# A gated cross-attention block on one core: softmax sums moved into the next group, longer due times for the feed-forward steps, a new order for the first sample and for the last group

## Chip, cores and metric

The kernel runs on one core of one Trainium2 chip. The metric is the device time of one execution in microseconds (us); lower is better. The kernel before was timed in three runs: 2811.11, 2811.09 and 2810.47 us, median 2811.09 us. One further execution was profiled; it took 2809.42 us, and its trace spans 2807.6 us from the first to the last instruction.

## What is computed

Four samples (B = 4) of 256 rows by 512 features (`x`) attend to 1601 context rows each (`ctx_kv`), then pass a feed-forward part with routed low-rank experts. Everything is float32.

```python
x = x + tanh(g_xattn) * xattn(layernorm(x), ctx, Wq, bq, Wkv, bkv, Wo, bo)
x = x + tanh(g_ffn)   * ffn(layernorm(x), base_W, router_W, lora_A, lora_B)

# xattn: 8 key/value heads, 4 query heads on each, head size 128
q = (query @ Wq + bq);  k, v = split(ctx @ Wkv + bkv)
attn = softmax(q k^T / sqrt(128));  out = (attn v) @ Wo + bo

# ffn: a base product and two of eight low-rank experts (rank 16)
probs = softmax(x @ router_W^T);  w = top-2 of probs, normalised
out = x @ base_W^T + 2 * sum_e w_e * (x @ lora_A_e) @ lora_B_e
```

## The kernel before

**Tiles.** A "head" below is one sample and one of its 8 key/value heads: 32 heads in all. Each head has two "groups" (`l` = 0, 1), of 128 rows of `x` with the 4 query heads that share the key: W = 512 columns. So there are 64 groups. The 1601 context rows are cut into 13 tiles of 128 rows (KT = 13); the last has 65 rows. For the softmax they are taken in 7 units (`pairs`): the 65-row tile alone first, then six units of two tiles.

**A group.** A score matmul (line 416, tile `sc`) multiplies the keys of one context tile with the 512 query columns. TensorE runs a float32 matmul in two passes, so 13 tiles are 26 matmul records. ScalarE copies each score tile from PSUM into an SBUF tile `p` (line 423), and VectorE folds the copies into a running maximum (`fold`, lines 373 to 378). `softmax` (line 430 on) then spreads the maximum over the partitions (`spread`), subtracts it from every `p` (line 437), lets ScalarE take the exponential (line 438), folds the running sum in the same loop, and spreads the sum's reciprocal. The value product (line 453, tile `av`) uses these `p` tiles in the next group's section: `run_group(cur, prev)` alternates score units of the current group with value units of the one before, which trail by AHEAD = 3 units. There are NBUF = NPAIR + AHEAD = 10 `p` tiles. VectorE multiplies the value product with the reciprocal sum (line 463), ScalarE adds the value bias (line 464), and an output projection (line 476, tile `po`) adds into the residual `xa`.

**Order of TensorE.** TensorE's order is written out by the program; the other engines' orders are chosen when the program is compiled. A small planner keeps a virtual clock (`clock["now"]`) that advances by an assumed cost for each TensorE step (`mm_cost`: 857 ns for a two-pass 512-column matmul). Work outside the score and value units is put into `Task` lists: key and query projections of the next head (`qk_steps`, tiles `pk` and `pq`), value projections (`v_steps`, tile `pv`), the output projection, the feed-forward steps, and transposes of the next sample's context. Each step has a cost and a lag: it is due only that long after the step ahead of it. `run_group` may run one due step of up to 432 ns after each unit; `fill`, after each group, runs due steps up to a share of what is left; `flush` runs a set to its end, and moves the clock forward where nothing is due. A lag that is too short lets TensorE reach an instruction whose input isn't there, and everything behind it in TensorE's queue waits.

**Feed-forward.** After a sample's last head, `ffn_steps` gives four steps for each 128-row part: a layer norm on VectorE (`fn`), its transpose on TensorE (`pt_f`, LAG_NORM = 6000 ns later), the router and expert product `pm` with a chain of about twenty small VectorE instructions that ends in `mid` (lines 524 to 548), and, LAG_ROUTE = 13000 ns later, `final_item`: the transpose of `mid` (line 558), the base product `py` (line 563) and the expert product into the same bank (line 564).

**Beginning and end.** The first sample's 13 context tiles are loaded into `p` tiles by SyncE's and ScalarE's DMA queues in turn, behind the biases and the first key weights; `x` goes in after the fourth. They are transposed (`pt_ctx`) and copied to `ctxT` by VectorE (line 143), layer norms of `x` come between, and the four blocks of key matmuls follow as their chunks are complete. The value projection follows the first group's scores. At the end the last group's value units run alone, after its softmax.

Of the kernel before, what the change touches and what calls it, by code (L numbers as in the profile page):

```python
# [27 lines left out]
def flamingo_kernel(  # L28
# [55 lines left out]
    AHEAD = 3  # L84
# [25 lines left out]
    nc.gpsimd.dma_start(gates[:, 0:1], g_xattn.partition_broadcast(P))  # L110
    nc.gpsimd.dma_start(gates[:, 1:2], g_ffn.partition_broadcast(P))
    nc.scalar.activation(gates, gates, AF.Tanh)
    tgx, tgf = gates[:, 0:1], gates[:, 1:2]
    bo_b = const.tile([P, D], F32, name="bo_b")
    nc.gpsimd.dma_start(bo_b, bo.partition_broadcast(P))
# [4 lines left out]
    nc.sync.dma_start(bias[0:NHEAD], bq.rearrange("(h p) -> h p", p=P))  # L120
    nc.sync.dma_start(bias[NHEAD:], bkv.rearrange("(h p) -> h p", p=P))
    biasT = const.tile([P, NBIAS], F32, name="biasT")
    pb = bank("pb")
    nc.tensor.transpose(pb[:, :NBIAS], bias, ident[:NBIAS, :NBIAS])
    nc.vector.tensor_copy(biasT, pb[:, :NBIAS])
# [12 lines left out]
    def transpose_rows(src, n, dst, name):  # L138

        pt = bank(f"pt_{name}").rearrange("p (c k) -> p c k", k=P)  # L140
        for c in range(NC):
            nc.tensor.transpose(pt[:, c, :n], src[:n, c * P : (c + 1) * P], ident[:n, :n])  # L142
        nc.vector.tensor_copy(dst, pt[:, :, :n])  # L143
# [23 lines left out]
    def load_wk(b, h):  # L167
        k = pool.tile([P, NC, HDIM], F32, tag="wk", name=f"wk_{b}_{h}")
        nc.sync.dma_start(
            k, wkv[:, h * HDIM : (h + 1) * HDIM].rearrange("(c p) f -> p c f", p=P)  # L170
        )
        w_t["k", b, h] = k

    def load_wv(b, hp):
        v = pool.tile([P, NC, 2 * HDIM], F32, tag="wv", name=f"wv_{b}_{hp}", bufs=1)
        lo = KVD + hp * 2 * HDIM
        nc.sync.dma_start(v, wkv[:, lo : lo + 2 * HDIM].rearrange("(c p) f -> p c f", p=P))
        w_t["v", b, hp] = v
# [47 lines left out]
    LAG_DMA, LAG_CTX, LAG_NORM, LAG_ROUTE = 2500, 1500, 6000, 13000  # L226
    LAG_EVAC, LAG_O, LAG_SOFTMAX = 1500, 6000, 12000
# [52 lines left out]
    def turn_ctx(b, i, src):  # L280
        transpose_rows(src, rows[i], ctxT_t[b][:, :, i * P : i * P + rows[i]], f"ctx_{b}_{i}")
# [120 lines left out]
    def score_unit(key, j):  # L402
# [4 lines left out]
        def run():  # L407
# [3 lines left out]
            p = pool.tile([P, 2, W], F32, tag="p", name=f"p_{nm}_{j}", bufs=NBUF)  # L411
# [16 lines left out]
    acc_t = {}  # L428

    def softmax(key):  # L430
        nm = "_".join(map(str, key))
        mb = spread(acc_t[key], ALU.max, f"mx_{nm}")
        sm = pool.tile([P, 2, W], F32, tag="sm", name=f"sm_{nm}", bufs=1)
        for j, tiles in enumerate(pairs):
# [4 lines left out]
            fold(sm, ALU.add, j, key)  # L439
        rb_t[key] = spread(sm, ALU.add, f"sm_{nm}", lambda m: nc.vector.reciprocal(m, m))  # L440
# [52 lines left out]
    def ffn_steps(b, l):  # L493
# [26 lines left out]
        def route_item():  # L520
            pm = bank(f"pm_{nm}")
            WR = E * R + E
            for c in range(NC):
                nc.tensor.matmul(
                    pm[:, :WR], box["xT"][:, c, :], ra[:, c, :], start=(c == 0), stop=(c == NC - 1)
                )
            lm = pool.tile([P, WR], F32, tag="lm", name=f"lm_{nm}")
# [28 lines left out]
        def final_item():  # L556
# [4 lines left out]
            py = bank(f"py_{nm}")  # L561
            for c in range(NC):
                nc.tensor.matmul(py, box["xT"][:, c, :], base_t[:, c, :], start=(c == 0), stop=False)  # L563
# [8 lines left out]
            (NC * mm_cost(E * R + E), LAG_EVAC, route_item),  # L572
            ((NC + 1) * mm_cost(D), LAG_ROUTE, final_item),
# [4 lines left out]
    NBUF = NPAIR + AHEAD  # L578
# [29 lines left out]
    def flush(which, until=math.inf):  # L608

        while left := [t for t in tasks if which(t)]:  # L610
            t = min(left, key=lambda t: max(t.ready, clock["now"]))
            if t.ready > until:
                break
# [3 lines left out]
    def run_group(cur, prev):  # L617
# [3 lines left out]
        for j in range(NPAIR + AHEAD):  # L621
            if cur is not None and j < NPAIR:
                units.append(score_unit(cur, j))
            if prev is not None and j >= AHEAD:
                units.append(av_unit(prev, j - AHEAD))
        for cost, fn in units:
            fn()
            clock["now"] += cost
            if (t := next_task(NC * TR_COST)) is not None:
                t.step()  # L630
# [3 lines left out]
    def fill(share, wait=LAG_EVAC):  # L634

        credit = share * sum(t.cost() for t in tasks)
        while tasks and credit > 0:
            if (t := next_task()) is None:
                soon = min(t.ready for t in tasks)
                if soon > clock["now"] + wait:  # L640
                    break
# [10 lines left out]
    load_wk(*heads[0])  # L652
    staged = {}
    for i in range(KT):
        eng = nc.sync if i % 2 == 0 else nc.scalar
        if i % 2 == 0:
            two = pool.tile([P, 2, W], F32, tag="p", name=f"ctx_0_{i}", bufs=NBUF)
        staged[i] = two[:, i % 2, :]
        eng.dma_start(staged[i][: rows[i]], ctx_kv[0, i * P : i * P + rows[i], :])
        if i == 3:  # L660
            xs = x_steps(0, 0)
            xs.pop(0)[2]()
    load_wq(*heads[0])
    load_wv(0, 0)
# [3 lines left out]
    done = 0  # L668
    for (s, n), k in zip(chunks, ks):
        while done * P < s + n:  # L670
            turn_ctx(0, done, staged.pop(done))
            done += 1
        if xs:
            for f in xs[:2]:
                f[2]()
            xs = xs[2:]
        k[2]()
    for f in qs:
# [4 lines left out]
    tasks.append(Task(v_steps(0, 0), (0, 0)))  # L683

    prev = None
    for hi, (b, h) in enumerate(heads):
# [9 lines left out]
        if nxt is not None:  # L696
            ks, qs = qk_steps(*nxt)
            if nxt[1] == 0:
                tasks.append(Task(ctx_steps(nxt[0]) + ks + v_steps(nxt[0], 0) + qs, nxt))
                tasks.append(Task(x_steps(nxt[0], LAG_NORM), nxt))  # L700
            else:
# [5 lines left out]
        for l in range(NL):  # L707
            cur = (b, h, l)
            fill(0)
# [4 lines left out]
            if hi == 0 and l == 0:  # L714
                flush(lambda t: t.head == heads[0])
                tasks.append(Task(ffn_weight_steps()))
            fill(1.0 / (NL - l), LAG_EVAC if nxt is not None else LAG_SOFTMAX)
# [3 lines left out]
    flush(lambda t: True, clock["now"] + LAG_SOFTMAX)  # L721
    run_group(None, prev)
    tasks.insert(0, Task(out_steps(prev)))
    flush(lambda t: True)
# [43 lines left out]
```

## Time and profile before

| what | value |
|---|---|
| median of three runs (range) | 2811.09 us (2810.47 to 2811.11) |
| the profiled execution / its span | 2809.42 us / 2807.6 us |
| TensorE (PE) busy, share of the span | 2708.2 us, 96% |
| VectorE (DVE) busy | 2034.1 us, 72% |
| ScalarE (ACT) busy | 1152.8 us, 41% |
| DMA over the span | 104.53 MB, mean 37 GB/s |
| mean granted TensorE clock | 0.986 |

How to read it: the page gives busy time per engine, the chain of work that ended last, and groups of instructions by source line. The list of waits says which engine stood before an instruction and what released it; the timeline lists instructions in order of time, where like ones are merged ("x4") with the start of the first and the time from there to the end of the last. A matmul's recorded end is modelled and overlaps the next one's start, so the spacing of starts is what counts. "PEld" is the load of the stationary operand. A busy TensorE can still be a slow one: its granted clock (1.00 is full) stands beside each window.

### The profile page before, as it was taken

To read this page: it belongs to the slowest core of one execution; us is meant where nothing else is said; L and a number is where in the kernel's file an instruction comes from. 1 tells how busy PE (TensorE), PEld (TensorE's weight loads), DVE (VectorE), ACT (ScalarE), POOL (GpSimd) and SP (SyncE) were. 2 spreads that over 40 slices of the span, in tenths; PEclk is the share of its full clock that TensorE was granted. 3 is DMA by queue.
4 is the path that set the end of the run, shared out by engine and by line. 5 is a ranking of instruction groups with operands and counts; after the bars stand their busy time and mean duration, and the time that the engine had idled before them with its cause. 6 is when DMAs were issued, how large, how long until landed. Compare 5 with 4: busy or idle time off the path is not lost.

```text
span 2807.6 us, 22670 instructions
## 1 busy us (share of the span) xinstructions
PE 2708.2 (96%) x7997; PEld 1469.5 (52%) x7997; DVE 2034.1 (72%) x3146; ACT 1152.8 (41%) x1769; POOL 6.2 (0%) x21
## 2 busy tenths in 40 slices
PE   7999999999899999999999999999999999999995
PEld 4655555555545555555544555555554455555542
DVE  4676777787658777768756787677866667777785
ACT  2443443443334434434433444344433434443442
POOL 0000000000000000000000000000000000000000
PEclk9999999999999999999999999999999999999997
DMA  4100010111101101102010111011210101110000
GB/s 149 42 34 27 34 34 23 42 53 47 45 26 37 39 19 42 34 23 71 29 45 27 42 34 34 27 34 38 61 36 23 36 25 34 41 34 15 31 15 8
DMA packets 69801, 104.53 MB, mean 37 GB/s; under 512 B 3068, under 2 KB 27692, under 8 KB 69688
## 3 DMA queue, kind: packets, MB, share of 16 engines
q1 hardware_dynamic: 68552, 100.99, 11.2%
q10 hardware_dynamic: 864, 1.57, 0.2%
q8 instruction: 63, 1.03, 0.1%
q0 software_dynamic: 272, 0.53, 0.1%
q14 instruction: 50, 0.41, 0.0%
HBM read 100.98 MB, written 2.10 MB: 37 GB/s over the span
## 4 chain that ended last, share of the span: by engine, by line
PE 86%; DVE 11%; issue 1%; ACT 1%; DMA 1%; ACTq 0%; DVEq 0%
PE sc L416 26%; PE av L453 23%; PE pv L347 11%; PE pk L295 10%; PE pq L314 7%; PE po L476 6%; DVE p L437 3%; DVE sm L378 2%; PE py L563 1%; ACT p L423 1%; DVE mx L378 1%; DVE sm L373 1%; DVE ctxT L143 0%; DMA xa<-in_x_dram 0%; PE pt_ctx L142 0%
## 5 line engine op out<-in xcount | busy, mean ns | idle before, releaser
L416 PE MATMUL sc<-qT,kT 128*128 128x512 f32 (+1 forms) x1664 | 783.8, 604 | 4.8 <-ACT qT L321 4.5
L453 PE MATMUL av<-p,v 128*128 128x512 f32 (+1 forms) x1664 | 759.3, 594 | 0.0
L423 ACT COPY p<-sc 128x512 f32<-128x512 f32 (+1 forms) x832 | 461.8, 587 | 710.1 <-PE av L453 607.0
L378 DVE TENSOR_TENSOR mx<-mx,p 128x1024 f32<-128x1024 f32 x256 | 313.3, 1224 | 442.2 <-ACT p L423 441.8
L453 PEld LDWEIGHTS av<-p,v 128*128 128x128 f32 (+1 forms) x1664 | 315.1, 191 | 386.9 <-issue 386.4
L416 PEld LDWEIGHTS sc<-qT,kT 128*128 128x128 f32 (+1 forms) x1664 | 292.5, 186 | 419.9 <-issue 273.8
L438 ACT ACTIVATE p<-p 128x1024 f32<-128x1024 f32 (+1 forms) x448 | 440.2, 994 | 127.1 <-DVE p L437 120.3
L437 DVE TENSOR_TENSOR p<-p,res_mx 128x1024 f32<-128x1024 f32 (+1 forms) x448 | 489.9, 1139 | 1.9
L347 PE MATMUL pv<-wv,ctxT 128*128 128x256 f32 (+1 forms) x1664 | 370.8, 380 | 0.0
L295 PE MATMUL pk<-ctxT,wk 128*128 128x400 f32 (+1 forms) x1024 | 357.3, 501 | 5.9 <-DVE ctxT L143 5.9
L347 PEld LDWEIGHTS pv<-wv,ctxT 128*128 128x128 f32 (+1 forms) x1664 | 310.2, 186 | 64.4 <-issue 15.3
L378 DVE TENSOR_TENSOR sm<-sm,p 128x1024 f32<-128x1024 f32 x256 | 311.9, 1218 | 11.2 <-ACT p L438 0.5
L295 PEld LDWEIGHTS pk<-ctxT,wk 128*128 128x128 f32 x1024 | 193.4, 190 | 167.5 <-issue 23.5
L476 PE MATMUL po<-wo,oT 128*128 128x512 f32 x512 | 233.8, 600 | 4.9 <-ACT oT L464 4.9
L314 PE MATMUL pq<-xnT,wq 128*128 128x256 f32 x1024 | 233.5, 382 | 0.0
L314 PEld LDWEIGHTS pq<-xnT,wq 128*128 128x128 f32 x1024 | 195.3, 191 | 43.5 <-issue 11.0
L464 ACT ACTIVATE oT<-oT,biasT 128x512 f32<-128x512 f32 x64 | 46.2, 722 | 371.6 <-DVE oT L463 371.6
L373 DVE TENSOR_TENSOR mx<-p,p 128x1024 f32<-128x1024 f32 x64 | 77.1, 1205 | 138.7 <-ACT p L423 138.7
L354 ACT COPY v<-pv 128x512 f32<-128x512 f32 (+1 forms) x112 | 61.7, 552 | 239.8 <-PE pv L347 239.8
L476 PEld LDWEIGHTS po<-wo,oT 128*128 128x128 f32 x512 | 98.2, 192 | 111.5 <-issue 94.6
L302 ACT ACTIVATE kT<-pk,biasT 128x400 f32<-128x400 f32 (+1 forms) x128 | 74.3, 584 | 74.7 <-PE pk L295 74.7
L321 ACT ACTIVATE qT<-pq,biasT 128x256 f32<-128x256 f32 x128 | 58.7, 463 | 61.3 <-PE pq L314 60.8
(96 smaller groups left out, 1124.9 us busy)
## 6 DMA issues: line engine op xcount, KB each, us to landing
wq<-in_L_xattn_Wq_dram SPq DMA_DIRECT2D x32, 1024.0 KB, 5.2
wo<-in_L_xattn_Wo_dram SPq DMA_DIRECT2D x32, 1024.0 KB, 5.1
ctx<-in_ctx_dram SPq DMA_DIRECT2D x42, 256.0 KB, 2.7
wk<-in_L_xattn_Wkv_dram SPq DMA_DIRECT2D x32, 256.0 KB, 3.1
wv<-in_L_xattn_Wkv_dram SPq DMA_DIRECT2D x16, 512.0 KB, 3.3
xa<-in_x_dram SPq DMA_DIRECT2D x4, 512.0 KB, 6.0
out_dram<-y SPq DMA_DIRECT2D x8, 256.0 KB, 2.6
ctx<-in_ctx_dram ACTq DMA_DIRECT2D x6, 256.0 KB, 5.1
```

The source lines that it names most:

```text
L295: nc.tensor.matmul(pk[:, :n], w_t["k", b, h][:, c, :], ctxT_t[b][:, c, s : s + n], start=(c == 0), stop=(c == NC - 1),)
L302: nc.scalar.activation(kT_t[b, h][:, s : s + n], pk[:, :n], AF.Identity, bias=bias_of("k", h),)
L314: nc.tensor.matmul(pq[:, :L], w_t["q", b, h][:, c, g * HDIM : (g + 1) * HDIM], xnT_t[b][:, c, :], start=(c == 0), stop=(c == NC - 1),)
L347: nc.tensor.matmul(pv[:r, j * WV : (j + 1) * WV], ctxT_t[b][:, c, s : s + r], w_t["v", b, hp][:, c, :], start=(c == 0), stop=(c == NC - 1),)
L373: nc.vector.tensor_tensor(acc, p[first], p[first + 1], op)
L378: nc.vector.tensor_tensor(acc, acc, p[j], op)
L416: nc.tensor.matmul(sc[:r, :], kT_t[b, h][:, i * P : i * P + r], qT_t[b, h][:, :, l * P : (l + 1) * P], start=True, stop=True,)
L423: nc.scalar.copy(p[:r, k, :], sc[:r, :])
L437: nc.vector.tensor_tensor(p, p, mb[:r].unsqueeze(1).to_broadcast([r, n, W]), ALU.subtract)
L438: nc.scalar.activation(p, p, AF.Exp, scale=scale)
L453: nc.tensor.matmul(av, v_t[b, h // 2][:r, i, h % 2, :], p_t[key][j][:r, k, :], start=(j == 0 and k == 0), stop=(j == NPAIR - 1 and k == le ...
L476: nc.tensor.matmul(po, oT_t[key][:, g, :], w_t["o", b, h][:, g, :], start=(g == 0), stop=(g == G - 1),)
```

## The change

It does five things; the matmuls, their sizes and their sums are the same as before.

1. **Sums.** `softmax` no longer folds the sums. `sum_unit(key, j)` does it, called in the next group's `run_group`: one fold ahead of each score unit, the spread with the seventh. AHEAD becomes 2, and NBUF = NPAIR + AHEAD + 1 stays 10.
2. **Lags and filling.** LAG_NORM 6000 to 12000, LAG_ROUTE 13000 to 25000; `route_item` comes LAG_COPY = 4000 after the transpose, in place of 1500. The base product moves from `final_item` to `route_item`, right behind `pm`. After a unit, steps of no cost no longer use up the turn. At a change of sample the task of `x` stands ahead of the context's, and the query projections ahead of the values.
3. **Context copies.** `ctxT` is copied out of PSUM by ScalarE, except the even tiles of the first sample, which stay with VectorE.
4. **First sample.** New load order (context tile 0 first on SyncE, key weights first on ScalarE, `x` behind the context); the biases are transposed after the third context tile; keys and values are projected tile by tile as the transposes go on; the layer norms of `x` come with the last four tiles; the base weights' task starts with the first group.
5. **End.** The last group's scores run right behind the group before it, into the space of `ctxT` (all units but the first); the last two groups' value units follow, the last with other due steps between them.

```diff
-    AHEAD = 3
+    AHEAD = 2
...
+    def load_small():
+        nc.sync.dma_start(bias[0:NHEAD], bq.rearrange("(h p) -> h p", p=P))
+        nc.scalar.dma_start(bias[NHEAD:], bkv.rearrange("(h p) -> h p", p=P))
+        nc.gpsimd.dma_start(gates[:, 0:1], g_xattn.partition_broadcast(P))
...
-    LAG_DMA, LAG_CTX, LAG_NORM, LAG_ROUTE = 2500, 1500, 6000, 13000
-    LAG_EVAC, LAG_O, LAG_SOFTMAX = 1500, 6000, 12000
+    LAG_DMA, LAG_CTX, LAG_NORM, LAG_ROUTE = 2500, 1500, 12000, 25000
+    LAG_EVAC, LAG_COPY, LAG_O = 1500, 4000, 6000
...
+            nc.vector.tensor_copy if b == 0 and i % 2 == 0 else nc.scalar.copy,
...
+            if key == last and j > 0:
+                if j == 1:
+                    flat = pool.tile([P, NC * LK], F32, tag="ctxT", name="p_last", bufs=1)
...
     def softmax(key):
...
             nc.scalar.activation(p, p, AF.Exp, scale=scale)
-            fold(sm, ALU.add, j, key)
-        rb_t[key] = spread(sm, ALU.add, f"sm_{nm}", lambda m: nc.vector.reciprocal(m, m))
+
+    def sum_unit(key, j):
+        nm = "_".join(map(str, key))
+        if j == 0:
+            acc_t[key] = pool.tile([P, 2, W], F32, tag="sm", name=f"sm_{nm}", bufs=1)
+        fold(acc_t[key], ALU.add, j, key)
+        if j == NPAIR - 1:
+            rb_t[key] = spread(
+                acc_t[key], ALU.add, f"sm_{nm}", lambda m: nc.vector.reciprocal(m, m)
+            )
...
+            py = bank(f"py_{nm}")
+            for c in range(NC):
+                nc.tensor.matmul(py, box["xT"][:, c, :], base_t[:, c, :], start=(c == 0), stop=False)
+            box["py"] = py
             lm = pool.tile([P, WR], F32, tag="lm", name=f"lm_{nm}")
...
-            (NC * mm_cost(E * R + E), LAG_EVAC, route_item),
-            ((NC + 1) * mm_cost(D), LAG_ROUTE, final_item),
+            (NC * (mm_cost(E * R + E) + mm_cost(D)), LAG_COPY, route_item),
+            (mm_cost(D), LAG_ROUTE, final_item),
...
-    NBUF = NPAIR + AHEAD
+    NBUF = NPAIR + AHEAD + 1
...
-        for cost, fn in units:
+        sums = list(range(NPAIR)) if prev is not None and not summed else []
+        for unit, key, j in units:
+            while sums and (unit is score_unit or sums[0] <= j):
+                sum_unit(prev, sums.pop(0))
+                if unit is score_unit:
+                    break
+            cost, fn = unit(key, j)
             fn()
             clock["now"] += cost
-            if (t := next_task(NC * TR_COST)) is not None:
-                t.step()
+            while (t := next_task(most)) is not None and not t.step():
+                pass
...
+    load_first(0)
+    load_wk(*heads[0], nc.scalar)
+    load_first(1)
+    load_first(2)
+    load_small()
+    load_first(3)
+    load_wv(0, 0)
+    for i in range(4, KT):
+        load_first(i)
...
+    for i in range(KT):
+        turn_ctx(0, i, staged[i])
+        if i == 2:
+            turn_bias()
...
+        if i >= KT - 4 and xs:
+            xs.pop(0)[2]()
+        if ends[0] <= i * P + rows[i]:
+            ends.pop(0)
+            ks.pop(0)[2]()
+        elif i > 3 and 2 * n_v + 1 <= i:
+            n_v += 1
+            vs.pop(0)[2]()
+    for f in xs + vs + qs:
+        f[2]()
...
-                tasks.append(Task(ctx_steps(nxt[0]) + ks + v_steps(nxt[0], 0) + qs, nxt))
                 tasks.append(Task(x_steps(nxt[0], LAG_NORM), nxt))
+                tasks.append(Task(ctx_steps(nxt[0]) + ks + qs + v_steps(nxt[0], 0), nxt))
...
-    flush(lambda t: True, clock["now"] + LAG_SOFTMAX)
-    run_group(None, prev)
+    for j in range(NPAIR):
+        sum_unit(prev, j)
+        cost, fn = score_unit(last, j)
+        fn()
+        clock["now"] += cost
+    softmax(last)
+    flush(lambda t: True)
+    run_group(None, prev, 0, summed=True)
     tasks.insert(0, Task(out_steps(prev)))
+    run_group(None, last, 0, math.inf)
+    tasks.insert(0, Task(out_steps(last)))
     flush(lambda t: True)
```

## The prediction

> **What bounds the kernel now.** I read the page's busy times first, then the list of waits, then the timeline of each kind of stage, and the windows for the clock.
>
> ```profile
> PE 2708.2 (96%) x7997; PEld 1469.5 (52%) x7997; DVE 2034.1 (72%) x3146; ACT 1152.8 (41%) x1769; POOL 6.2 (0%) x21
> ```
>
> TensorE bounds the kernel. What can be won is its idle time, 2807.6 - 2708.2 = 99.4 us, and the time in which it counts as busy but goes slowly. The list of waits has one that recurs in every group:
>
> ```profile
> ACT p L423 <- PE av L453: 607.0, 252, 3.2
> ...
> PEld sc L416 <- ACT p L423: 132.4, 199, 1.0
> ```
>
> The timeline of TensorE in a steady group, then of ScalarE there, shows what that is:
>
> ```profile
> 1036.35 2.02 PE L416 MATMUL sc<-qT,kT 128*128 128x512 f32 x4
> 1038.20 1.88 PE L453 MATMUL av<-p,v 128*128 128x512 f32 x4
> 1039.92 2.02 PE L416 MATMUL sc<-qT,kT 128*128 128x512 f32 x4
> 1041.78 1.88 PE L453 MATMUL av<-p,v 128*128 128x512 f32 x4
> ```
>
> ```profile
> 1040.17 1.07 ACT L423 COPY p<-sc 128x512 f32<-128x512 f32 x2 [2.50 <-PE av L453]
> ```
>
> Four value matmuls take 1039.92 - 1038.20 = 1.72 us (0.43 each), four score matmuls 1.85 or 1.86: 0.14 us more, though both have 512 columns. The copy of a score waits for the value unit *behind* it: with 10 `p` tiles and 7 units, the copy of unit j writes the tile that value unit j - 3 of the group before reads, and AHEAD = 3 puts that unit behind score unit j. The three `sc` banks then run short, and the next weight load waits for ScalarE. 199 times 0.14 = 28 us.
>
> Second, the change of sample; the waits of TensorE alone between 560 and 860 us, and the timeline at the longest:
>
> ```profile
> PE pmt L558 <- DVE mid L548: 6.9, 1, 6.9
> PE pt_f L142 <- DVE quadm_sm L391: 3.7, 1, 3.7
> PE pt_f L142 <- DVE fn L155: 3.1, 1, 3.1
> PE sc L416 <- ACT qT L321: 1.1, 2, 0.6
> PE pk L295 <- DVE ctxT L143: 1.0, 1, 1.0
> ```
>
> ```profile
> 817.79 0.45 PE L558 MATMUL pmt<-ident,mid 128*128 128x128 f32 x1 [6.87 <-DVE mid L548]
> 818.03 5.84 PE L563 MATMUL py<-base_t,fT 128*128 128x512 f32 x8
> ```
>
> 15.8 us of waits, and the same again at the next two changes. After a wait the clock is lower: these eight `py` take 5.84 us, eight at full clock 3.60 (2777.32 us).
>
> Third, the first 22 us, and fourth, the end:
>
> ```profile
> 11.74 1.28 ACT L152 ACT_TABLE_LOAD   x1 [11.74 <-DMA ctx<-in_ctx_dram]
> 16.49 1.29 DVE L147 BATCH_NORM_STATS2 st_x<-xa 128x6 f32<-128x512 f32 x2 [16.49 <-DMA xa<-in_x_dram]
> 18.22 1.12 PE L142 MATMUL pt_ctx<-ident,ctx 128*128 128x128 f32 x4 [5.02 <-DVE sd_x L151]
> 21.25 4.22 PE L295 MATMUL pk<-ctxT,wk 128*128 128x401 f32 x8
> ...
> 2759.70 1.12 PE L142 MATMUL pt_f<-ident,fn 128*128 128x128 f32 x4 [13.96 <-DVE fn L155]
> 2763.98 13.39 PE L453 MATMUL av<-p,v 65*128 65x512 f32 x26
> ```
>
> At the beginning VectorE's queue stands behind the layer norm of `x` until `xa` lands at 16.49, and the context copies behind it with it; real work starts at 21.25. At the end TensorE has nothing while the last softmax runs.
>
> **A. The ring of p tiles: -25 us.** With AHEAD = 2 and still 10 tiles, copy j needs value unit j - 3, which now stands directly *ahead* of score unit j. The wait goes, and with it up to 28 us. What takes its place: tile j - 3 must also have been read by its sum fold, which now runs in the same section. Tiles 0 to 2 are read by the fold of unit 2, which VectorE can do before the section, and later folds precede their use by three units. In one two-tile unit (3.43 us of TensorE) VectorE has a maximum and a sum fold, 1.14 us of spacing each, and ScalarE two copies, 1.07 us. It fits. The sum's spread (a chain of small instructions, 4.3 us) stands ahead of the last maximum fold; it moves that fold and the exponentials by at most 4.3 us, but leaves the subtractions sooner done, as 10.8 us of sum work between and behind them is gone. The first exponential is needed some 20 us after the last score (a fill of 16 to 21 us, three score units), and is there after about 9. Ends: 0 (something else holds the copies; a loss only by the last rival) and 28; I take 25, nine tenths, for groups in which ScalarE or VectorE is late.
>
> **B. Change of sample: -52 us.** Does the new lag cover each wait? The projection that ended at 700.66 had its `fn` at 711.3, 10.6 us later; the one that ended at 758.1 at 769.2, 11.1 us. The lag was 6, now 12. From the end of `pm` at 795.2 to `mid` at 817.7 are 22.5 us; the lag was 13, now 25, and VectorE's share in between shrinks, as sum folds stood between the chain's instructions. So 6.9 + 3.7 + 3.1 go; the query wait (1.1) goes mostly, as value projections now stand between the queries and the scores. The clock's loss goes with them: `py` 2.2, the scores behind it 6.53 against 6.17, `pt_f` 1.09 against 0.60, `pm` 1.58 against 1.09: 3.6 us. Sum 19.4. I leave 2 standing: the key wait of 1.0 (now for ScalarE's copy), and 1 where the routing follows its transpose so closely that `fT` isn't copied. Three times 17.4 = 52; ends 15 (half covered, clock still lost) and 58. What it costs: `py` holds one of four `ps` banks for 25 us or more. A key block takes 2.7 us and its eviction 0.6, so three banks still turn in time: 0. Forty-five context copies go from VectorE (0.68) to ScalarE (0.58 for the same shape), at 41% busy: 0. The steps themselves are the same matmuls, later: 0, as long as projections (16 to 21 us in each fill) are there to stand in front of them; without that cover a lag of 25 us would be a wait of 25.
>
> **C. First sample: -7 us.** Before, from the first key block (21.25) to the end of the value projection (82.50) TensorE was nearly without a gap, and the same work stands there after, in another order; two or three waits of about 1 us for a copy remain, as before (0.67, 1.20, 1.03). So what counts is when the first key block starts. It needs four tiles, the key weights, and ScalarE's copies of tiles 1 and 3, which stand in ScalarE's queue behind its own eight DMA issues (six before). A tile on ScalarE's queue landed 3.3 us after its issue, tile 0 behind the weights on SyncE's after 8.2 (2.11 to 10.35). By these rows, moving the key weights to ScalarE's queue would have everything there by 6 us, and the block at 8: -13. The Trainium skill speaks against it: "DMA: Bandwidth & Descriptors", Rules for kernel authors, says that spreading DMAs over the issuing engines brings no bandwidth, as all share the same 16 engines, and saves only issue time. Then bytes decide. ScalarE's last issues waited for earlier transfers before (the fifth at 10.35, when tile 0 landed), and will now wait for the value weights: about 2.1 MB with what shares the engines, which at the 191 GB/s of the first 10 us is 11 us. Add the table load (1.28) and two copies (0.58 each): the block starts at about 14, so -7. I take this, since the ScalarE row (table load only at 11.74, right behind its DMA issues) is nearest. Ends: -13, and -2 if ScalarE gets free later. A loss is excluded down to a key block at 21: `x` and its layer norm no longer stand ahead of any context copy. The other moved DMAs (biases, gates, `bo`) are needed at the first key eviction or later; behind tile 2 they land before it.
>
> **D. End: -20 us.** Before: 2684.4 to 2807.6. After, scores of the first last-head group start at the same point; with the value units they are 52 matmuls = 22.3 us, to 2706.7. The last scores follow at once (26 x 0.43 = 11.2, to 2717.9), one projection (3.4), the value units (11.2, to 2732.5). VectorE is now what is late. From the maximum of that group (2706.5): spread 4.2, `oT` 0.6, subtractions 7.4, sums 6.3 with spread 4.5, maxima of the last group 6.3, residual 0.7, `oT` 0.6, spread 4.2: 2741.3, and the first exponential at 2742.5. So TensorE is idle some 10 us there. Then 26 value matmuls with one projection between, 14.6, and 2 for the lowered clock (before, these 26 took 13.39 in place of 11.2): 2759. The last sums end at 2761.4, `oT` with its bias at 2763; projection to 2766.5; the other part's transpose, `pm` and base product to 2772.6; then this part's transpose, copy, `pm`, base product (2778.4), the first part's last product, `mid` (4.4 after `pm`, as at 2791.9 to 2796.3: 2780.4), last product 2782. The two parts' results share one `xn` tile, so the second waits for the first one's store (2.6): end near 2787. 2807.6 - 2787 = 20. Ends: 10 and 26.
>
> **Sum.** 25 + 52 + 7 + 20 = 104 us; 2809.4 - 104 = 2705.4 for an execution like the profiled one. The runs' median lies 1.7 above it: **2707 us**. From the other side: at full clock a sample's matmuls are 980 of 512 columns at 0.43 us, 672 of 256 at 0.216, 256 of 400 at 0.336 and 10 us of transposes and routing, 662 in all, 2648 for four; add 14 at the beginning, 5 of small waits there and of cold clock, about 34 idle at the end, 6 at the changes of sample: 2707 by this way.
>
> **Rivals.**
> *The ring still waits* (0.14). ScalarE's order is chosen at compile time; if copies stand behind exponentials or a sum fold, A is lost: 2707 + 25 = 2732. For it: 132 us of ScalarE waits and the fuller VectorE section; against: the unit's arithmetic above.
> *The lags miss half* (0.11): a wait only moves to the next step, or to the bank that `py` holds; B gives 15 to 26: 2733 to 2744. Against: all three waits are shorter than the added lags, 6 and 12 us.
> *Both, or the end is bound by VectorE as before* (0.06): about 2760.
> *Slower than before* (0.03): VectorE and TensorE lock step through the ring. If a sum fold were queued behind a maximum fold of a later unit, copy j would wait for that fold and TensorE for the copy; four units of each of 62 groups can lock. One unit's chain is two copies, a maximum and a sum fold, 1.07 + 1.14 + 1.14 = 3.35 us, against 3.43 of TensorE; it decides from 0.42 us over that, as 0.42 x 4 x 62 = 104 eats the gain. At 1 us it gives 2707 + 248 = 2955. The DVE rows speak against it, as they leave 0.08.
> *As forecast* (0.66): 2690 to 2722, from the ends of C and D and small misses in A and B.
>
> **Numbers.** The range is 2690 to 2742: the likeliest case, the first rival and most of the second. What a measurement of this kernel can tell from no change is about 0.2%, 5.6 us: faster 0.95, within 0.02, slower 0.03.
>
> **What would show it.** A: score units spaced 1.72 us, and the weight load's wait for line 423 near zero (wrong: still 199 of them). B: no wait over 1.5 us for `mid` or `fn` at the changes of sample, `py` x8 at 3.6. C: first `pk` near 14 us. D: last projection near 2763 less what was won earlier, an idle stretch of about 10 us before the last value units. The forecast is wrong if VectorE's or ScalarE's queue order brings a new wait into each group; one of 0.4 us a group is already 25 us.

## The result

| | before | after |
|---|---|---|
| median (range) | 2810.78 us (2810.38 to 2811.11) | 2764.52 us (2761.53 to 2765.00) |
| ratio, 95% interval | | 0.9833 [0.9816, 0.9850] |
| profiled execution / span | 2809.42 / 2807.6 us | 2761.53 / 2759.7 us |
| mean granted TensorE clock | 0.986 | 0.988 |

The change is faster by 46 us, 1.7%; the forecast was 104 us (2707, range 2690 to 2742). The page's busy line after:

```profile
PE 2674.3 (97%) x7997; PEld 1480.7 (54%) x7997; DVE 2008.3 (73%) x3101; ACT 1178.3 (43%) x1811; POOL 6.2 (0%) x21
```

TensorE's busy time fell by 34 us, its idle time by only 14 (99.4 to 85.4). To see which stage gave what, the table compares the start of the same instruction in both traces:

| point | before | after | gain so far |
|---|---|---|---|
| first key block of the second head | 82.50 | 81.48, with 1.3 us of base-weight transposes ahead of it that stood later in the kernel before | 2.3 |
| scores of the first sample's last head, first group | 616.30 | 608.97 | 7.3 |
| scores of the second sample's third head, first group | 910.46 | 899.76 | 10.7 |
| scores of the last sample's last head, first group | 2684.41 | 2655.32 | 29.1 |
| end of the span | 2807.6 | 2759.7 | 47.9 |

Two heads without a change of sample, four groups, went from 162.45 to 160.78 us: 0.42 a group. Fourteen groups of the first sample gave 7.3 - 2.3 = 5.0, 0.36 a group. Six groups lie around the first change of sample. At 0.42 each they should give about 2.5 us, and the stretch gave 3.4: the change of sample itself gave **0.9 us, where 17.4 were forecast**. The sum by stage: 2 (beginning) + 24 (62 groups) + 3 (three changes of sample) + 19 (end, 123.2 to 104.4) = 48.

The 2 us of the beginning belong to this one execution: it took 2761.53 us, the three others of the change 2764.42 to 2765.00. In the eight experiments that keep this beginning as it is, the first point of the table stands at 83.17 to 84.50. Less the 1.3 us that is 81.9 to 83.2, no clear gain over 82.50.

**Steady groups.** TensorE's timeline after, in a group of the second sample. Score and value units now both stand 1.72 us apart:

```profile
810.53 1.88 PE L435 MATMUL sc<-qT,kT 128*128 128x512 f32 x4
812.25 1.88 PE L482 MATMUL av<-p,v 128*128 128x512 f32 x4
813.97 1.88 PE L435 MATMUL sc<-qT,kT 128*128 128x512 f32 x4
```

In the list of waits, ScalarE's copy now waits for the score that it copies, and no longer for the value unit behind it:

```profile
ACT p L442 <- PE sc L435: 610.4, 817, 5.4
```

**Change of sample.** TensorE's waits between 560 and 900 us of the changed kernel:

```profile
PE py L595 <- DVE midT L593: 14.2, 2, 9.2
PE po L505 <- ACT qT L330: 0.9, 1, 0.9
...
```

The waits for `fn` and `mid` are gone, and the wait for `midT`, which I had not looked at, stands in their place: 16.2 us with the small ones, 15.8 before. Over the whole span it is 44.6 us in 8 waits. TensorE's timeline at the waits of both parts, then VectorE's in the same stretches:

```profile
779.93 0.27 PE L591 MATMUL pmt<-ident,mid 128*128 128x128 f32 x1
785.24 2.08 PE L595 MATMUL py<-lb,midT 128*128 128x512 f32 x2 [5.03 <-DVE midT L593]
787.10 2.92 PE L323 MATMUL pq<-xnT,wq 128*128 128x256 f32 x8
...
827.70 0.27 PE L591 MATMUL pmt<-ident,mid 128*128 128x128 f32 x1
837.16 2.08 PE L595 MATMUL py<-lb,midT 128*128 128x512 f32 x2 [9.19 <-DVE midT L593]
```

```profile
777.29 7.48 DVE L457 TENSOR_TENSOR p<-p,res_mx 65x512 f32<-65x512 f32 x7
...
784.90 0.28 DVE L593 COPY midT<-pmt 128x128 f32<-128x128 f32 x1
...
829.42 7.48 DVE L457 TENSOR_TENSOR p<-p,res_mx 65x512 f32<-65x512 f32 x7
836.83 0.28 DVE L593 COPY midT<-pmt 128x128 f32<-128x128 f32 x1
```

In the kernel before, VectorE's timeline has the second part's copy right behind the transpose at 817.79, in a queue that had nothing else to do:

```profile
818.28 0.29 DVE L560 COPY midT<-pmt 128x128 f32<-128x128 f32 x1 [0.63 <-PE pmt L558]
```

This is the reading of the case. `final_item` holds a transpose, a copy on VectorE and a product that needs the copy, one right behind the other. TensorE's transpose at 779.93 has its input. But the copy of 0.28 us stands in VectorE's queue behind the seven subtractions of the softmax, 7.48 us, that begin at the end of each group. The second part's copy (836.83) stands behind the next group's seven, which run from 829.42 to 836.90. TensorE waits for each copy, and so does everything behind it in its queue. The clock's loss is there again too: the windows give a granted clock of 0.58 from 785 to 790 us (1.00 from 775 to 780), and eight `pq` take 2.92 us. The next eight, at 793.29, take 1.89.

**Beginning.** TensorE's timeline of the changed kernel, then ScalarE's (the last five of its six context loads are issued from 2.27 to 10.16), then VectorE's:

```profile
12.61 2.96 PE L304 MATMUL pk<-ctxT,wk 128*128 128x401 f32 x8 [1.73 <-ACT ctxT L146]
...
23.71 5.41 PE L356 MATMUL pv<-wv,ctxT 128*128 128x256 f32 x16 [3.81 <-ACT kT L311]
...
32.99 2.93 PE L304 MATMUL pk<-ctxT,wk 128*128 128x400 f32 x8 [3.43 <-DVE mv_x L152]
```

```profile
10.19 1.28 ACT L146 ACT_TABLE_LOAD   x1 [10.19 <-DMA ctx<-in_ctx_dram]
...
22.83 0.34 ACT L155 ACTIVATE sd_x<-sd_x 128x1 f32<-128x1 f32 x2 [8.88 <-DVE sd_x L154]
23.08 0.58 ACT L311 ACTIVATE kT<-pk,biasT 128x401 f32<-128x401 f32 x1
```

```profile
30.96 1.29 DVE L150 BATCH_NORM_STATS2 st_x<-xa 128x6 f32<-128x512 f32 x2 [5.76 <-DMA xa<-in_x_dram]
32.17 0.67 DVE L146 COPY ctxT<-pt_ctx 128x512 f32<-128x512 f32 x1
```

The first key block starts at 12.61. But its eviction, the copy out of PSUM (`kT`, 23.08), stands in ScalarE's queue behind the square root of the layer norm, which waits for `xa`. On VectorE the statistics of the *second* sample's `x` stand at 30.96 ahead of a context copy and wait for their own load. TensorE waits 3.81 and 3.43 us for these two. The program issues both norms later than these copies; the compiled order put them ahead.

**End.** TensorE's waits in its timeline from 2684 us on, in the changed kernel:

```profile
2684.02 1.12 PE L435 MATMUL sc<-qT,kT 128*128 128x512 f32 x2 [1.57 <-ACT p_last L442]
2687.43 7.73 PE L435 MATMUL sc<-qT,kT 128*128 128x512 f32 x14 [2.28 <-ACT p_last L442]
...
2716.55 2.04 PE L482 MATMUL av<-p,v 65*128 65x512 f32 x2 [6.78 <-DVE oT L492]
...
2735.18 3.70 PE L505 MATMUL po<-wo,oT 128*128 128x512 f32 x8 [1.54 <-ACT oT L493]
```

The longest waits before (13.96 and 2.99 for `fn`, 4.38 for `mid`) have given way to 1.57 + 2.28 + 6.78. The 6.78 has the form of the waits for `midT`. The multiplication `oT` must empty the one `av` bank before the last value units can start. It stands in VectorE's queue behind six of the last group's subtractions:

```profile
2708.91 6.89 DVE L457 TENSOR_TENSOR p_last<-p_last,res_mx 128x1024 f32<-128x1024 f32 x6
2715.72 0.68 DVE L492 TENSOR_TENSOR oT<-av,res_sm 128x512 f32<-128x512 f32 x1
```

No run moved it.

### The profile page after: what moved, and what is told of

Its sections match the earlier page's. It is cut to its first block, busy times and chain, and to the rows that moved or that the text cites. A ratio compares the mean times of both kernels' runs of the same rounds, so it can differ in the third digit from the quotient of the medians.

```text
span 2759.7 us, 22496 instructions
## 1 busy us (share of the span) xinstructions
PE 2674.3 (97%) x7997; PEld 1480.7 (54%) x7997; DVE 2008.3 (73%) x3101; ACT 1178.3 (43%) x1811; POOL 6.2 (0%) x21
## 3 DMA queue, kind: packets, MB, share of 16 engines
q8 instruction: 63, 1.03, 0.2%
## 4 chain that ended last, share of the span: by engine, by line
PE 91%; DVE 6%; ACT 2%; DMA 1%; issue 1%; SPq 0%; ACTq 0%; DVEq 0%
PE sc L435 26%; PE av L482 23%; PE pv L356 13%; PE pk L304 12%; PE po L505 8%; PE pq L323 8%; DVE p L457 2%; ACT p L458 1%; DVE mx L387 1%; DMA ctx<-in_ctx_dram 1%; PE py L558 0%; PE py L595 0%; PE pt_ctx L145 0%; DVE mx L392 0%; DVE res_mx L406 0%
## 5 line engine op out<-in xcount | busy, mean ns | idle before, releaser
L435 PE MATMUL sc<-qT,kT 128*128 128x512 f32 (+1 forms) x1664 | 768.9, 593 | 6.7 <-ACT p_last L442 3.9
L482 PE MATMUL av<-p,v 65*128 65x512 f32 x1640 | 756.8, 593 | 6.8 <-DVE oT L492 6.8
L442 ACT COPY p<-sc 65x512 f32<-65x512 f32 x820 | 479.4, 585 | 610.5 <-PE sc L435 610.4
L482 PEld LDWEIGHTS av<-p,v 65*128 65x128 f32 x1640 | 310.1, 190 | 389.4 <-issue 377.5
L435 PEld LDWEIGHTS sc<-qT,kT 128*128 128x128 f32 (+1 forms) x1664 | 307.7, 186 | 382.6 <-issue 360.9
L457 DVE TENSOR_TENSOR p<-p,res_mx 65x512 f32<-65x512 f32 x442 | 472.2, 1135 | 0.1
L458 ACT ACTIVATE p<-p 65x512 f32<-65x512 f32 x442 | 421.3, 990 | 40.4 <-DVE p L457 34.2
```

What stands on the lines that cost most here:

```text
L435: nc.tensor.matmul(sc[:r, :], kT_t[b, h][:, i * P : i * P + r], qT_t[b, h][:, :, l * P : (l + 1) * P], start=True, stop=True,)
L442: nc.scalar.copy(p[:r, k, :], sc[:r, :])
L457: nc.vector.tensor_tensor(p, p, mb[:r].unsqueeze(1).to_broadcast([r, n, W]), ALU.subtract)
L458: nc.scalar.activation(p, p, AF.Exp, scale=scale)
L482: nc.tensor.matmul(av, v_t[b, h // 2][:r, i, h % 2, :], p_t[key][j][:r, k, :], start=(j == 0 and k == 0), stop=(j == NPAIR - 1 and k == le ...
```

## The experiments

Theory 1 of this document: the time was lost at the change of sample, because the copy of `midT` stands behind the softmax's subtractions; the ring and the end are worth what the prediction said. The rivals, tested one by one below, are the missing cover of the base product, the lags themselves, the moved sums, and the latency through PSUM on whichever engine. An expectation's own "theory 1" can be another one. Ratios are to the kernel before, timed beside each run (medians 2810.7 to 2811.6 us).

**1. The copy ahead of its product (`e1_split`).** Transposing `mid` and copying it become a step of their own, and the product comes 10 us later. Same matmuls.

```diff
-        def final_item():
+        def mid_item():
             pt = bank(f"pmt_{nm}")
             nc.tensor.transpose(pt[:, :P], box["mid"], ident)
-            midT = pool.tile([P, P], F32, tag="midT", name=f"midT_{nm}", bufs=1)
+            midT = pool.tile([P, P], F32, tag="midT", name=f"midT_{nm}", bufs=2)
             nc.vector.tensor_copy(midT, pt[:, :P])
+            box["midT"] = midT
+
+        def final_item():
             py = box["py"]
...
-            (mm_cost(D), LAG_ROUTE, final_item),
+            (TR_COST, LAG_ROUTE, mid_item),
+            (mm_cost(D), 10000, final_item),
```

> The changed kernel, with the last feed-forward step cut in two: the transpose of mid and its copy are a step of their own (25 us after the routing), and the expert product comes 10 us later. Theory 1 (moving the base product away uncovered the copy of midT, which stands in VectorE's queue behind up to seven subtractions): the wait of 5.0 + 9.2 us for midT at each change of sample goes, the lowered clock behind it (about 4 us) too, so the time falls by 3 x 18 = 54 us and 2 at the end, from 2764 to about 2709; no wait of TensorE over 1.5 us is left at a change of sample. Theory 2 (it is the longer lags and the bank that the base product holds, and the wait only shows itself at midT): the wait comes back at another instruction and the time stays above 2745.

2720.17 us (2719.62 to 2721.09), ratio 0.9676 [0.9660, 0.9692]: 44 us less than the change, where some 56 were expected. TensorE's timeline at the second part, VectorE's there, then TensorE's waits between 560 and 900 us:

```profile
812.40 0.27 PE L591 MATMUL pmt<-ident,mid 128*128 128x128 f32 x1
...
826.24 1.02 PE L598 MATMUL py<-lb,midT 128*128 128x512 f32 x2
```

```profile
812.71 0.29 DVE L593 COPY midT<-pmt 128x128 f32<-128x128 f32 x1
...
827.97 7.48 DVE L457 TENSOR_TENSOR p<-p,res_mx 65x512 f32<-65x512 f32 x7
```

```profile
PE po L505 <- ACT p L458: 2.4, 1, 2.4
...
```

The copy stands 15 us ahead of the subtractions, and 16.2 us of waits become 4.3. One small new wait (2.4) came in at each change: an output projection for ScalarE. From the scores of the first sample's last head to those of the second sample's third head, the trace takes 275.4 us (611.99 to 887.40), against 290.8 in the change and 294.2 before. Less the 2.5 us of its six groups, this change of sample gives 16.3 of the 17.4 that were forecast.

The kernel's text says why the step stood where it did. `run_group` takes a step between two units only if its cost is at most 432 ns. `final_item` costs 857, so it must wait until the group is over, just where the softmax has put its subtractions into VectorE's queue. The transpose alone costs 108 and goes between two units, as at 812.40.

**2. The base product as a cover again (`e2_base_back`).** In the change, but with the base product between the transpose and the expert product, as before.

```diff
-            (NC * (mm_cost(E * R + E) + mm_cost(D)), LAG_COPY, route_item),
-            (mm_cost(D), LAG_ROUTE, final_item),
+            (NC * mm_cost(E * R + E), LAG_COPY, route_item),
+            ((NC + 1) * mm_cost(D), LAG_ROUTE, final_item),
```

> The changed kernel, with only the base product put back behind the transpose of mid, as before the change. Theory 1: its 3.4 us cover the copy again, but the block of subtractions is 7.4 us long now, where it was cut up by sum folds before; 5.0 - 3.4 and 9.2 - 3.4 remain, 7.4 of 14.2 us at each change of sample, so the time falls by about 3 x 8 = 24 to 2740. Theory 2: within 6 us of 2764.

2762.83 us, ratio 0.9825 [0.9811, 0.9840]: no different from the change, so the expected 2740 was a miss. The waits for `midT` fall to 32.4 us (5.03 and 5.76 at a change of sample): the cover takes its 3.4 us off the longer one. Other waits come in for it, two of 2.6 for the queries among them. The stretch of experiment 1 takes 288.8 us against 290.8, and the end 106.9 against 104.4. Moving the base product is not where the time went.

**3. The old lags with the split (`e3_old_lags`).** Experiment 1 with both lags as before.

```diff
-    LAG_DMA, LAG_CTX, LAG_NORM, LAG_ROUTE = 2500, 1500, 12000, 25000
+    LAG_DMA, LAG_CTX, LAG_NORM, LAG_ROUTE = 2500, 1500, 6000, 13000
```

> e1_split with the old lags, 6 us for the norm and 13 for the routing. If the longer lags are worth what the forecast said, the waits for fn (3 to 4 us, twice) and for mid (7) come back: e1_split plus about 3 x 14, some 42 us slower than e1_split. If the moved sums alone made these chains short enough, it is within 8 us of e1_split.

2749.23 us, ratio 0.9781 [0.9766, 0.9795]: the lags are worth 29 us once the copy is out of the way, between the two expectations. The waits for `fn` (5.3 in two) and `mid` (3.0) are back at the first change of sample, but shorter than those of the same steps in the kernel before (6.8 and 6.9). So part of what the prediction gave to the lags comes with the rest of the change.

**4. Only the last lag undone (`e10_route_13`).** The change with LAG_ROUTE 13000, copy and product still in one step.

```diff
-    LAG_DMA, LAG_CTX, LAG_NORM, LAG_ROUTE = 2500, 1500, 12000, 25000
+    LAG_DMA, LAG_CTX, LAG_NORM, LAG_ROUTE = 2500, 1500, 12000, 13000
```

> The change with one number undone: the lag ahead of the last feed-forward step is 13000 ns again instead of 25000, all else as in the change, copy and product in one step. Theory 1 (the longer lag itself puts that step behind the softmax's subtractions in VectorE's queue; with the shorter one the copy stands right behind the routing's last operation): the waits of py for midT fall from 44.6 us to under 10, waits of pmt for mid of 2 to 6 us per boundary come back, 2735 us (2722 to 2746). Rival (a short lag only turns the wait for midT into one for mid as long as the one before, 7 us and more a boundary, with the copy's own wait behind it): 2750 us or more.

2737.17 us, ratio 0.9737 [0.9721, 0.9754]. VectorE's timeline: the copy stands right behind the last operations of the routing and the spread of the sums.

```profile
805.66 0.24 DVE L581 TENSOR_TENSOR mid<-lm,wd 128x128 f32<-128x128 f32 x1
...
807.13 0.25 DVE L593 COPY midT<-pmt 128x128 f32<-128x128 f32 x1
```

The waits for `midT` fall to 6.4 us over the span; those of the same step for `mid` and for the spread ahead of it are 14.9. So with copy and product in one step the longer lag cost 27 us: it carried the step from a place where its input was a little late to the end of a group, where its copy stands behind a long block.

**5. The copy on ScalarE (`e12_mid_act`).**

```diff
-            nc.vector.tensor_copy(midT, pt[:, :P])
+            nc.scalar.copy(midT, pt[:, :P])
```

> The change with the copy of midT on ScalarE instead of VectorE, nothing else. Theory 1 (the wait is the place in VectorE's queue): in ScalarE's queue the second part's copy stands ahead of the exponentials, the first part's behind six of seven of them, so the longer wait of each boundary (9.2 us) goes and the shorter (5.0) stays: 44.6 us of waits fall to 15 to 21, 2738 us (2732 to 2745). Rival (the wait is the latency from the transpose through PSUM to the product, on whichever engine the copy is): 2760 to 2768 us.

2732.59 us, ratio 0.9722 [0.9707, 0.9736]. ScalarE's timeline at the two parts:

```profile
781.66 5.36 ACT L458 ACTIVATE p<-p 65x512 f32<-65x512 f32 x6
786.93 0.24 ACT L593 COPY midT<-pmt 128x128 f32<-128x128 f32 x1
...
829.81 0.27 ACT L593 COPY midT<-pmt 128x128 f32<-128x128 f32 x1 [4.73 <-PE pmt L591]
```

The first part's copy stands behind six exponentials and its wait stays (4.8 us). The second part's finds ScalarE free, and 0.4 us is left of its wait. The waits for `midT` are 16.4 us in all. It is the place in the queue, not the way through PSUM.

**6. The sums back in the softmax (`e9_sums_back`, the change; `e5_sums_back`, experiment 1).** The folds stand behind each exponential again; AHEAD and the ten tiles stay.

```diff
             nc.scalar.activation(p, p, AF.Exp, scale=scale)
+            sum_unit(key, j)
...
-        sums = list(range(NPAIR)) if prev is not None and not summed else []
+        sums = []
```

> The change with one part undone: the folds of the sums stand in the softmax again, behind each pair's exponential. Theory 1 (the moved sums are at fault: they close the block of seven subtractions, and the copy of midT stands behind it): the waits of py for midT fall from 44.6 us to under 20, and the time falls below 2750 even though the ring's part is partly lost. Theory 2 (the place is at fault: the longer lag puts the step that holds copy and product together at the end of a group, so the copy stands behind the subtractions whether sums lie among them or not): the waits stay at 40 us or more and the time is 2764 to 2795, since the block in front of the copy is now longer by the folds.

> The first experiment's kernel (2720.17 us, no waits for midT left) with the folds of the sums in the softmax again. Theory 1 (the ring of tiles and the shorter lead give the saving; the folds' place matters only where a copy stands behind them): 2723 us (2719 to 2728), score and context units still about 1.72 us apart. Rival (moving the sums out is itself worth what the change's time lost when they went back, about 24 us): 2738 us or more.

In the change: 2788.64 us, ratio 0.9921 [0.9906, 0.9936], and the waits for `midT` are 65.5 us instead of 44.6, as the second theory of the expectation had it. VectorE's timeline just ahead of the copy, and the wait that follows on TensorE:

```profile
836.52 5.21 DVE L457 TENSOR_TENSOR p<-p,res_mx 65x512 f32<-65x512 f32 x5
...
845.66 1.22 DVE L387 TENSOR_TENSOR sm<-sm,p 128x1024 f32<-128x1024 f32 x1
846.79 0.28 DVE L594 COPY midT<-pmt 128x128 f32<-128x128 f32 x1
```

```profile
847.12 2.08 PE L596 MATMUL py<-lb,midT 128*128 128x512 f32 x2 [12.06 <-DVE midT L594]
```

The block ahead of the copy is longer by the folds. With the copy out of the way (`e5_sums_back`): 2716.43 us, ratio 0.9664 [0.9650, 0.9678], against 0.9676 [0.9660, 0.9692] with the sums moved: no difference that these runs can tell. So moving the sums, the change's first part, has no gain of its own in these runs; what it gave here was a shorter block ahead of `midT`.

**7. The ring alone (`e4_ring_only`).** The kernel before with two numbers changed.

```diff
-    AHEAD = 3
+    AHEAD = 2
...
-    NBUF = NPAIR + AHEAD
+    NBUF = NPAIR + AHEAD + 1
```

> The kernel before with two of its numbers changed: score units run two ahead of the context units (3 before) and the ring of score tiles holds one tile more. Theory 1 (the ring's share is a plain removal, independent of the rest): a unit of a group falls by 0.05 to 0.08 us in the 15 full groups, the wait of the score matmul for a free tile shrinks, 2784 us (2781 to 2790). Rival (the ring's gain needs the sums out of the softmax, since the folds still stand among the subtractions and hold the tile): less than a third of it, 2800 to 2811.

2791.67 us, ratio 0.9934 [0.9919, 0.9949]: 20 us from two numbers, between theory 1 of the expectation (27) and its rival. In its list of waits ScalarE's copy waits for its score alone:

```profile
ACT p L423 <- PE sc L416: 628.3, 822, 2.9
```

The ring no longer holds it. In the trace the fourteen groups of the first sample (83.44 to 612.24) give 5.0 us, as much as in the change. The rest was lost at the changes of sample. The stretch of experiment 1 takes 296.5 us here against 294.2 before, though its six groups should have saved 2.5. TensorE's list of waits is 11 us longer than before, and `py` waits for `midT`, 25.9 us in three, are new. The longest at the first change is 8.6 us, and its copy (754.13) stands behind subtractions and folds that start at 743.85. So with steps that merely shifted in time, the same wait came while the lags and the sums were as before.

**8. The old beginning, and the norms held back (`e6_head_old`, `e8_norm_held`, both on experiment 1).** `e8_norm_held` keeps the new beginning, but puts the layer norms of `x` into the queues behind context copies of VectorE and ScalarE. Its edit (`behind` holds the latest context copy of each engine):

```diff
-                layernorm(xn, xa_t[b][:, l, :], f"x_{b}_{l}")
+                with tc.issue_after(behind[0]), tc.issue_after(behind[1]):
+                    layernorm(xn, xa_t[b][:, l, :], f"x_{b}_{l}")
```

The edit of `e6_head_old` puts back the old loads and loops, and all context copies of the first sample on VectorE:

```diff
-    load_first(0)
-    load_wk(*heads[0], nc.scalar)
...
+    load_small()
+    turn_bias()
+    nc.scalar.activation(gates, gates, AF.Tanh)
+    load_wk(*heads[0])
+    staged = {}
+    for i in range(KT):
...
```

> The first experiment's kernel (transposing mid a step of its own) with the beginning of the kernel before: loads, first K, norm and first V in the old order. Theory 1 (the reordered beginning is worth what the two traces show at the end of the first V, about 1 to 2.3 us, because the norms were pulled ahead of the copies that K and V wait for): 2722 us (2719 to 2725). Rival (it is worth the 7 us of the prediction, the rest being lost elsewhere): 2727 us or more.

> e1_split, with the layer norms of x queued behind the context copies that the program puts ahead of them, in VectorE's and ScalarE's order. Theory 1 for the beginning (the compile-time order put the norm's statistics and its root ahead of context copies and evictions, so both queues stood until x had landed): the waits of 3.8 us (values) and 3.4 us (second key block) go with the cold clock behind them, 8 to 9 us faster than e1_split. Rival (the bytes come too late, whatever the order): TensorE then waits for context tiles in their place and the gain is under 3 us.

Old beginning: 2720.17 us, ratio 0.9679 [0.9665, 0.9694], the same as the new one. The new order as compiled is worth nothing. Norms held: 2710.35 us, ratio 0.9641 [0.9627, 0.9655], 9.8 us less than experiment 1. ScalarE's timeline with the norms held:

```profile
17.00 0.60 ACT L315 ACTIVATE kT<-pk,biasT 128x401 f32<-128x401 f32 x1 [4.77 <-PE pk L308]
```

The first key eviction comes at 17.00 instead of 23.08. The waits of TensorE for `kT` (0.9 us in experiment 1) and for `mv_x` (5.1) are gone, and the second head's first key block starts at 74.55 instead of 84.50. The order of the program had a gain of the forecast size in it; the compiled queues had taken it away.

**9. The old end (`e7_tail_old`, on experiment 1).**

```diff
-    for j in range(NPAIR):
-        sum_unit(prev, j)
-        cost, fn = score_unit(last, j)
-        fn()
-        clock["now"] += cost
-    softmax(last)
-    flush(lambda t: True)
-    run_group(None, prev, 0, summed=True)
+    flush(lambda t: True, clock["now"] + LAG_SOFTMAX)
+    for j in range(NPAIR):
+        sum_unit(prev, j)
+    run_group(None, prev, summed=True)
```

> The first experiment's kernel with the end of the kernel before: the last group's scores in the ring, no early scores. Theory 1 (the end is worth what the end segments of the two traces differ by, 18.8 us, and is independent of the rest): 2739 us (2736 to 2742). Rival (part of that came from work that was moved ahead of the end and is paid there): 2726 to 2733.

2729.20 us, ratio 0.9709 [0.9693, 0.9725]: the new end is worth 9.0 us, not 18.8, a miss. The old end takes 114.5 us in this kernel and took 123.2 before: about half of the gain seen at the end comes from other parts of the change. Its longest wait, `pt_f` for `fn`, is 10.44 instead of 13.96, and that for `mid` 1.04 instead of 4.38.

**10. Both savings (`e13_both`).** `e8_norm_held` with the sums in the softmax, except for the last group but one.

```diff
+            if key != (B - 1, NKV - 1, 0):
+                sum_unit(key, j)
```

> The first experiment's kernel with the layer norms of the beginning held behind the context copies and, but for the last group but one, the folds of the sums in the softmax again. If the two savings are independent: 2720.2 less 9.8 (the held norms) less 3.7 (the sums back) less up to 4 (the wait of the last context units for oT at 6.5 us instead of 10.4) = 2703 to 2707 us. Rival (the sums' 3.7 us was within the scatter between calls and the folds back in the softmax bring nothing): 2710 us or more.

2709.72 us, ratio 0.9638 [0.9625, 0.9652], against 0.9641 [0.9627, 0.9655] for `e8_norm_held`: no difference, as the rival had it (2710 or more). These two are the fastest versions, some 54 us below the change.

## Why the prediction was wrong

The direction was right, the size wrong by a factor of two, and almost all of the error lies in one step.

*A, the ring: -25 forecast, about -24 measured.* Right, by its own mechanism: 0.36 to 0.42 us a group. The worked unit chain held, and no lock step came. What I had not seen is that the sums' move, which I spent most care on, isn't needed for it: two numbers alone give the same 5.0 us in fourteen groups (experiments 6 and 7).

*B, the change of sample: -52 forecast, -3 measured.* This is the step that failed. I asked "Does the new lag cover each wait?" for the waits that the trace of before showed, and it does: none for `fn` or `mid` is left, and the eight `py` take 3.60 us, as the forecast's signs asked. Then I wrote "The steps themselves are the same matmuls, later: 0, as long as projections (16 to 21 us in each fill) are there to stand in front of them". The projections were there, and the step still cost 5.03 + 9.19 us of waiting at each change. A step is more than matmuls: its copy of 0.28 us enters VectorE's queue at another place. Before, the first part's copy (749.85) came ahead of the subtractions and the second's (818.28) long after them, with 3.6 and 5.8 us of base product over them. At the new time it stands behind 7.48 us of subtractions, and the sum had no term for it. The cover alone would not have helped (experiment 2); the place in the queue decides (experiments 1, 4 and 5). The rival "the lags miss half: a wait only moves to the next step" named this, but at 15 to 26 us left to win, where 3 were. With the copy placed earlier the change of sample gives 16.3 of its 17.4 us (experiment 1), so the arithmetic of the waits was sound, though not all of it is due to the lags (29 us in experiment 3).

*C, the beginning: -7 forecast, -2 in the profiled execution, 0 by experiment 8.* The first key block was forecast at 14 and came at 12.61, with ScalarE's queue free at 10.19 against 11. By the rows of single loads it would have been 8, so the rule that the prediction took agrees with this row; no run tested it alone. The failed sentence is "`x` and its layer norm no longer stand ahead of any context copy". That holds in the program's order; in the compiled order they do stand ahead, and waits of 3.81 and 3.43 us came in place of the "two or three waits of about 1 us". Held back, the beginning gives 9.8.

*D, the end: -20 forecast, -18.8 measured.* Right in size, and the last projection came at 2735.2 (2763 less the 29.1 won earlier is 2733.9). But the way there is in part luck. The idle stretch ahead of the last value units is 6.78 us, not "some 10", and it ends with the multiplication `oT`, not with the first exponential, which is over at 2709.7. The last scores, which were to "follow at once", lose 1.57 + 2.28 us to ScalarE's copies. And experiment 9 gives the new order only 9.0 of the 18.8; the rest came to the old order too, which the sum against the trace of before could not show.

The sum of what the forecast missed: 49 (B) + 5 (C) + 1 (A) + 1 (D) = 56, which is 104 - 48 of the profiled executions. The third rival's "about 2760" is close to the result only by chance: its ring no longer waited, and its end was not as before.

## What to carry to other kernels

When a step of TensorE is moved in time, look up what the other engines have in their queues at the new time: a copy of 0.28 us between two matmuls cost 5 to 9 us each time, because it landed behind 7.48 us of subtractions. A TensorE step that goes out to another engine and comes back should be two steps with a lag between; a lag ahead of both covers nothing inside. And where queues are ordered at compile time, the order of the program proves nothing about them: read each engine's own timeline, and undo the parts of a change one by one. Read more than one execution, too: the 2 us of the beginning were in one trace and not in eight others.

## What the runs showed of the hardware

A wait costs more than its length once it is long. From 832 to 837 us, late in the 9.19 us wait, the granted clock is 0.50, from 837 to 842 it is 0.66, then 1.00. The two `py` behind the wait take 2.08 us, against 1.02 without one. After the wait of 2.41 us in experiment 1 the projection takes 3.67 against 3.60. The Trainium skill's page "TensorE: Matmul & The Clock Gate", What's actually happening, says that the clock is halved after at least one idle window of about 3.4 us and comes back after at least one busy window of that length; these rows agree. They put some 4 us on each change of sample (2 x 1.06 for `py`, 1.03 for `pq`, 0.7 for the keys), about as much as the 3.6 before.
